# VectorE's order behind the next unit's maxima, and half of a layer's maxima moved into its attention

## The chip, the cores and the metric

The kernel runs on one core of a Trainium2 chip. A core has five engines with a queue each: TensorE (PE for its matmuls, PEld for the loads of their stationary operand), VectorE (DVE), ScalarE (ACT), GpSimd (POOL) and SyncE (SP). SP and POOL also issue the DMAs here. The metric is the device time in microseconds; the kernel before takes 2418.72 us, the median of three runs (2417.28 to 2425.54).

## The reference

Four blocks of attention, one after the other, work on x, 4 sequences of 1024 tokens with 256 channels, and on a context of 4 times 77 tokens. All is float32.

- L0 (16 heads of 16 channels): layer norm, self attention under a mask, residual; layer norm, attention to the context, residual; layer norm, a feed-forward of 1024 channels with relu, residual. Under the mask only a few keys at the end of a sequence take part.
- L1 (4 heads of 64 channels), three layers: the first attends to the context, the second and third to x itself, 1024 queries by 1024 keys. Each is

```
Q, K, V = relu(q @ Wq + bq), relu(k @ Wk + bk), relu(v @ Wv + bv)
attn    = softmax(Q K^T / 8) * query_mask
out     = layer_norm(attn V + q)
x       = leaky_relu(out @ Wff + bff, 0.2) + out
```

- L2 and L3 (16 heads of 16 channels): attention to the context, residual and layer norm; L2 has an output projection, L3 has none.

A softmax needs the maximum of each row of scores before the exponentials.

## The kernel before

**Items and units.** Each layer is run for one sequence after the other; a layer and a sequence is an item. Seven layers make 28 items: `SelfFew` (self attention of L0, when at most 32 keys count), `Cross16` (attention to the context with 16 heads: "ca" of L0, "l2", "l3"), `Cross4` (first layer of L1), `Self4` (second and third layer of L1). An item's attention is a row of units: 4 in SelfFew, 8 in Cross16 and Cross4, 16 in Self4.

**The order of PE.** PE runs in the order in which the program is written. That order is made by `Pipe` and `Pump`. In each unit `Pipe.unit` calls what is due as "full", then the unit's scores, then what is due as "next", then the pump, then what is due as "turn", "late" and "col". The pump fills a unit with steps from two lists: the first holds the start of the next item (norms, transposes to channels, queries, maxima), the second the end of the item before (projection, residual, norm, feed-forward). Each step has a cost of about its PE time, a lag (so much other cost shall pass before the list's next step) and at times a test. `Pump.__call__` takes the list that is further behind, and stops when the unit has its share or when neither list is ready. In an item's last unit it takes all that is left, lags or not. `Pump.until` takes steps of the first list, without regard to lags, until a test holds: an item's attention calls it before the units of each half of the tokens, so that the half's start is there. The other engines have no written order: a planner puts each of their instructions in a queue's order, by when it finds them ready and by the order of the program.

**Self4, the stage from 930 to 1884 us.** A unit is 128 queries and a pair of heads against 1024 keys. `Self4.scores`: PE writes two score tiles `ss` (two PSUM banks each; there are two such buffers, so the next unit's scores wait until this unit's are read), DVE takes the negative maximum of each (line 1241), ACT the exponentials with it into PR (line 1247). PR has two buffers, and each holds a pair of units. `turned_by_blocks` is called as "next", one unit later: DVE transposes the unit's part of PR in blocks of 32 by 32 (line 1259), and after the second unit of a pair 16 DMAs, 8 on SP's queue and 8 on POOL's, move the blocks into PT (line 1266). Two and three units after that `weighted` multiplies with V (line 1302) from PT.

**Cross16.** An item's `start` makes a list: for each half c of the tokens a norm where the layer has one, two transposes (`turn`), two queries, eight `maxima` (line 270 on PE into two PSUM tiles, line 275 on DVE), then `shift`. A maximum is needed per head and query so that the exponentials cannot overflow; `shift` splits it into three bf16 parts with four DVE instructions (lines 304 to 307) and lets PE transpose these (line 310), whose copy SH is added into the scores by a small matmul (line 352). `have_half` then counts the half. The scores of a unit are lines 346 and 352, the exponentials 356, the weighting 365, the transposes back 377. The PSUM pool "p1" for all these small tiles has four buffers. `SelfFew` inherits `shift` and has its own maxima (lines 917 and 921). The normalized x lies in a tile of tag "F", of which there is one; norms of both lists use it.

Of the kernel before, what the change touches and what calls it, by code (L numbers as in the profile page):

```python
# [13 lines left out]
ALU = mybir.AluOpType  # L14
# [69 lines left out]
class Pump:  # L84
# [31 lines left out]

    def until(self, test):
        while not test():
            self.take(0)


class Pipe:
# [26 lines left out]
    def run(self, items):  # L149
        pump = Pump(self, 1, items[0].start(), [])  # L150
        pump.until(lambda: items[0].halves >= 1)
        left = pump.lists[0]
        before = None
        for a, b in zip(items, items[1:]):
            b.prev = a
        for i, item in enumerate(items):
            last = i + 1 == len(items)
            first = left + ([] if last else items[i + 1].start())
            second = (before.end() if before else []) + (item.end() if last else [])
            left = []  # L160
            idle = item.idle()
            self.pump = pump = Pump(self, item.units + idle, item.more() + first, second)
            for _ in range(idle):
                self.unit()
            for scores in item.attend():
                self.unit(scores, item.cost)
            before = item
        while self.due:
            pump.n = 0
            self.unit()  # L170
        pump.n = pump.units - 1
        pump()


class Item:
# [4 lines left out]

    def more(self):

        return []

    def idle(self):

# [2 lines left out]
    def __init__(self, net, layer, b):  # L189
        self.net, self.l, self.b = net, layer, b  # L190
        self.halves, self.ended = 0, 0
        self.prev, self.later_half = None, True

    def room(self):

# [9 lines left out]
class Cross16(Item):  # L205
# [7 lines left out]
    def start(self):  # L213
# [23 lines left out]
        def norm(c):  # L237
            if l.norm is None:
                self.xn = x[:, 4 * c : 4 * c + 4, :]
                return  # L240
            mv, rstd = self.mv, self.rstd
            self.xn = net.tile("F", [P, 4, C], name="xn")
            for i in range(4):
                t = 4 * c + i
                nc.vector.tensor_scalar(
                    self.xn[:, i, :], x[:, t, :], mv[:, t, 0:1], rstd[:, t : t + 1], ALU.subtract, ALU.mult
                )

        def turn(c, cc):
            pt = net.p1.tile([P, 512], F32, tag="p1", name="pt")  # L250
            for i in range(4):
                nc.tensor.transpose(pt[:, ts(i, P)], self.xn[:, i, ts(cc, P)], net.ident)
            at = None if l.norm is None else COL_LN + 4 * (l.norm - 1) + cc
            g, be = (None, None) if at is None else (net.cols[:, at : at + 1], net.cols[:, at + 2 : at + 3])
            net.evac(self.hT[:, cc, ts(c, 512)], pt, g, be)

        def query(e, c):
            pp = net.p1.tile([P, 512], F32, tag="p1", name="pp")
# [19 lines left out]

        ln = l.norm is not None
        step(0, new, lag=8 * ln)  # L280
        for c in range(2):
            step(0, norm, c, lag=3 * ln)
            step(0.5, turn, c, 0)
            step(0.5, turn, c, 1, lag=2)
            if c == 0:
                step(0, new_q, test=self.room)
            for e in range(2):
                step(1.8, query, e, c)
            for e in range(2):
                for i in range(4):  # L290
                    step(0.55, maxima, e, 4 * c + i, lag=3 if (e, i) == (1, 3) else 0)
            step(0.3, self.shift, c)
            step(0, self.have_half)
        return steps

    def shift(self, c):

        net, h = self.net, H16
        nc = net.nc
        m = self.mx[:, 4 * c : 4 * c + 4, :].rearrange("p t (j g) -> p t j g", j=4)  # L300
        m3, rest = net.m3[c], net.rest16[c]
        parts = [m3.rearrange("p t (j r) -> p t j r", j=4)[:, :, :, i : 3 * G : 3] for i in range(3)]
        left = rest.rearrange("p t (j g) -> p t j g", j=4)
        nc.vector.tensor_copy(parts[0], m)
        nc.vector.tensor_tensor(left, m, parts[0], ALU.subtract)
        nc.vector.tensor_copy(parts[1], left)
        nc.vector.tensor_tensor(parts[2], left, parts[1], ALU.subtract)
        pm = net.p1.tile([P, 512], BF16, tag="p1", name="pm")
        for i in range(4):
            nc.tensor.transpose(pm[:, ts(i, P)], m3[:, i, :], net.identb)  # L310
        net.evac(self.sh[:, c, :], pm)

    def shift_by_row(self, c):
# [217 lines left out]
class Feed:  # L531
# [15 lines left out]
    def steps(self, b):  # L547
# [9 lines left out]

        def norm(c):
            s["xn"] = net.tile("F", [P, 4, C], name="xn")
            for i in range(4):  # L560
                t = 4 * c + i
                nc.vector.tensor_scalar(
                    s["xn"][:, i, :], x[:, t, :], s["mv"][:, t, 0:1], s["rstd"][:, t : t + 1], ALU.subtract, ALU.mult
                )

        def turn(c, cc):
# [2 lines left out]
                nc.tensor.transpose(pt[:, ts(i, P)], s["xn"][:, i, ts(cc, P)], net.ident)  # L569
            at = COL_LN + 8 + cc  # L570
            net.evac(s["hT"][:, cc, ts(c, 512)], pt, net.cols[:, at : at + 1], net.cols[:, at + 2 : at + 3])

        def hidden(q, f):

# [28 lines left out]
            step(0, self.load)  # L603
        step(0, new, lag=8)
        for c in range(2):
            step(0, norm, c, lag=3)
            step(0.5, turn, c, 0)
            step(0.5, turn, c, 1, lag=2 * c)
        for q in range(4):
# [24 lines left out]
class Self16(Cross16):  # L634
# [8 lines left out]
    def start(self):  # L643
# [18 lines left out]

        def norm(c):
            self.xn = net.tile("F", [P, 4, C], name="xn")
            net.normal(self.xn, x, self.mv, self.rstd, c)

        def turn(c, cc):
            net.turn_normal(self.hT, self.xn, 1, c, cc)

        def query(g, c):  # L670
            pp = net.p1.tile([P, 512], F32, tag="p1", name="pp")
# [49 lines left out]
        step(0, new, lag=8 if b else 0)  # L721
        for c in self.cs:
            if b:
                step(0, norm, c, lag=3)
                step(0.5, turn, c, 0)
                step(0.5, turn, c, 1, lag=2)
            step(1.8, query, 0, c)
# [100 lines left out]
class SelfFew(Cross16):  # L828
# [5 lines left out]
    def start(self):  # L834
# [21 lines left out]

        def norm(c):
            self.xn = net.tile("F", [P, 4, C], name="xn")
            net.normal(self.xn, x, self.mv, self.rstd, c)

        def turn(c, cc):
            net.turn_normal(self.hT, self.xn, 1, c, cc)

        def query(e, c):
            pp = net.p1.tile([P, 512], F32, tag="p1", name="pp")
# [57 lines left out]
        step(0, new, lag=8 if b else 0)  # L923
        for c in self.cs:
            if b:
                step(0, norm, c, lag=3)
                step(0.5, turn, c, 0)
                step(0.5, turn, c, 1, lag=2)
            if c == 1:
# [3 lines left out]
            if c == 1:  # L933
                step(0.9, values)
            for t in range(4 * c, 4 * c + 4):
                step(0.9, maxima, t, lag=3 if t % 4 == 3 else 0)
            step(0.3, self.shift, c)
            step(0, self.have_half)
        return steps
# [149 lines left out]
class Self4(Item):  # L1089
# [133 lines left out]
    def scores(self, p, t):  # L1223
# [14 lines left out]
        for h in range(2):  # L1238
            at = slice(2 * p + h, 2 * p + h + 1)
            s2 = ss[h].rearrange("p k n -> p (k n)")  # L1240
            nc.vector.tensor_reduce(self.nm[:, t, at], s2, AX.X, ALU.max, negate=True)  # L1241
            if net.blocks:
                out = self.pr[:, t % 2, h, :].rearrange("p (c k i) -> p k c i", c=4, i=32)
                s2 = s2.rearrange("p (k c i) -> p k c i", c=4, i=32)
# [8 lines left out]
    def turned_by_blocks(self, p, t, pr):  # L1253
# [2 lines left out]
        net = self.net  # L1256
        nc = net.nc
        part = pr[:, t % 2].rearrange("p h s -> p (h s)")
        nc.vector.transpose(part, part)  # L1259
        if t % 2 == 0:  # L1260
            return

# [189 lines left out]
class Net:  # L1452
    def __init__(self, ctx, tc, t):
        self.ctx, self.tc, self.nc, self.t = ctx, tc, tc.nc, t
        self.flip = 0

    def evac(self, out, src, scale=None, bias=None):

# [694 lines left out]
```

## Time and profile before

The profiled execution took 2419.14 us, with a span of 2417.3 us from its first to its last instruction, and a mean granted clock of PE of 0.951.

| stage, us from the start | length | PE busy | DVE busy | ACT busy | PE clock | DMA share |
|---|---|---|---|---|---|---|
| 0 to 40: load, first norm | 40 | 13.10 | 19.85 | 8.33 | 0.81 | 0.47 |
| 40 to 244: SelfFew | 204 | 182.59 | 127.31 | 42.52 | 0.97 | 0.09 |
| 244 to 686: Cross16 "ca" and feed-forward | 442 | 423.00 | 202.73 | 134.05 | 0.99 | 0.03 |
| 686 to 930: Cross4, with the last feed-forward | 244 | 216.96 | 135.78 | 108.14 | 0.91 | 0.02 |
| 930 to 1884: Self4, two layers | 954 | 902.51 | 782.49 | 445.23 | 0.97, 0.98 | 0.65, 0.69 |
| 1884 to 2417: Cross16 "l2" and "l3" | 533 | 458.28 | 313.93 | 190.62 | 0.89 | 0.05 |

Busy time is the union of an engine's instructions in microseconds. PE's is not work at full pace: the end of a matmul is modelled, so one that waits inside counts as busy. A line of the profile names the source line, the engine and the operation, the tiles as out<-in, the number of instructions, then their busy time, the mean of one in ns, and the idle time of the engine before them with what ended it. A line of the waits names who waited, for whom, how long in all, how often and the longest. The clock is the share of full speed that PE was granted.

### The profile page before, as it was taken

How to read it: one execution, taken by the hardware profiler on the slowest of the kernel's cores; microseconds unless marked ns; L12 is line 12 of the kernel's file. 1: busy time of each engine (PE TensorE's matmuls, PEld its weight loads, DVE VectorE, ACT ScalarE, POOL GpSimd, SP SyncE). 2: the span in 40 equal slices, each digit the busy share in tenths (PEclk: the TensorE clock that was granted, in tenths of full speed). 3: DMA queues.
4: the chain of work that ended last, by engine and by line, in shares of the span. 5: the costliest groups of instructions: out<-in, count | busy, mean ns of one | idle time of the engine just before them, and what ended most of it. 6: DMA issues, size and time to landing. Idle time of an engine off the chain costs nothing. (4 is left out here: it accounts for less than half of the span.)

```text
span 2417.3 us, 31250 instructions
## 1 busy us (share of the span) xinstructions
PE 2196.4 (91%) x11035; PEld 1226.0 (51%) x11035; DVE 1582.1 (65%) x3170; ACT 928.9 (38%) x1828; POOL 382.3 (16%) x652
## 2 busy tenths in 40 slices
PE   4899999999999979999998999999999899898886
PEld 2556546666768645545443545444444444444331
DVE  5566655444233666888889688878887655655665
ACT  1222342222332545544444445444443343333333
POOL 2000000000000000333333233333232100000000
PEclk8999999999989989999999999999999898998888
DMA  4000010000000001677667576666785300000000
GB/s 128 18 1 16 5 35 1 1 7 5 7 5 3 1 5 34 149 160 151 144 144 159 120 149 146 148 148 146 154 156 111 70 5 1 5 1 1 27 18 28
DMA packets 148550, 158.01 MB, mean 65 GB/s; under 512 B 51489, under 2 KB 130658, under 8 KB 148386
## 3 DMA queue, kind: packets, MB, share of 16 engines
q1 hardware_dynamic: 121842, 85.31, 16.6%
q0 software_dynamic: 25488, 69.56, 12.8%
q8 instruction: 91, 1.49, 0.3%
q10 hardware_dynamic: 1056, 1.05, 0.1%
q14 instruction: 73, 0.60, 0.1%
HBM read 17.41 MB, written 4.19 MB: 9 GB/s over the span
## 5 line engine op out<-in xcount | busy, mean ns | idle before, releaser
L1247 ACT ACTIVATE PR<-ss,nm 128x1024 f32<-128x1024 f32 x256 | 284.8, 1114 | 381.1 <-DVE nm L1241 294.4
L1259 DVE STREAM_TRANSPOSE PR<-PR 128x2048 f32<-128x2048 f32 x128 | 295.8, 2311 | 130.4 <-ACT PR L1247 115.5
L1266 POOL DMA_DIRECT2D PT<-PR x512 | 279.8, 554 | 591.9 <-PE ss L1230 227.9
L1230 PE MATMUL ss<-QK 64*128 64x512 f32 x1024 | 322.9, 630 | 26.3 <-ACT PR L1247 26.1
L1241 DVE TENSOR_REDUCE nm<-ss 128x1 f32<-128x1024 f32 x256 | 299.7, 1210 | 20.0 <-PE ss L1230 19.9
L1302 PE MATMUL po<-PT,V 128*64 128x256 f32 x2048 | 252.4, 389 | 2.3 <-DVE mx L275 2.2
L356 ACT ACTIVATE PT<-pb 77x1024 f32<-77x1024 f32 x192 | 185.4, 1016 | 178.4 <-PE pb L352 178.4
L275 DVE TENSOR_REDUCE mx<-pa 128x4 f32<-128x308 f32 x384 | 156.0, 469 | 71.2 <-PE pa L270 70.6
L1230 PEld LDWEIGHTS ss<-QK 64*128 64x128 f32 x1024 | 112.7, 188 | 172.0 <-ACT PR L1247 94.5
L270 PE MATMUL pa<-KA,QT 64*128 64x308 f32 x768 | 167.2, 490 | 30.2 <-DVE mx L275 29.8
L1302 PEld LDWEIGHTS po<-PT,V 128*64 128x64 f32 x2048 | 137.1, 138 | 106.1 <-issue 46.3
L365 PE MATMUL po<-PT,Vc 77*32 77x512 f32 x768 | 136.8, 652 | 18.5 <-ACT PT L356 9.6
L270 PEld LDWEIGHTS pa<-KA,QT 64*128 64x128 f32 x768 | 101.5, 197 | 97.3 <-DVE mx L275 45.4
L1509 POOL TENSOR_TENSOR pw<-va,minus_half 128x4 f32<-128x4 f32 (+1 forms) x28 | 38.0, 1358 | 619.7 <-DVE va L1507 542.0
L1469 ACT COPY OT<-po 128x512 f32<-128x512 f32 x57 | 33.4, 587 | 231.2 <-PE po L365 217.5
L346 PE MATMUL pb<-QT,KA 32*77 32x512 f32 x768 | 114.5, 668 | 0.0
L595 PE MATMUL pp<-w,hid 128*128 128x256 f32 x512 | 114.0, 381 | 0.0
L580 PE MATMUL pp<-hF,w 128*128 128x256 f32 x512 | 113.2, 379 | 0.0
L595 PEld LDWEIGHTS pp<-w,hid 128*128 128x128 f32 x512 | 96.5, 190 | 15.9 <-DVE mx L275 2.5
L580 PEld LDWEIGHTS pp<-hF,w 128*128 128x128 f32 x512 | 97.1, 190 | 14.6 <-issue 1.3
L1500 DVE BATCH_NORM_STATS2 st<-x 128x6 f32<-128x256 f32 x256 | 97.7, 405 | 5.6 <-DMA x<-in_x 4.4
L1373 PE MATMUL pp<-wo,hE 128*128 128x256 f32 x384 | 96.4, 393 | 1.6 <-ACT hE L1476 1.5
(257 smaller groups left out, 3147.3 us busy)
## 6 DMA issues: line engine op xcount, KB each, us to landing
PT<-PR SPq DMA_DIRECT2D x512, 128.0 KB, 5.5
PT<-PR POOLq DMA_DIRECT2D x512, 128.0 KB, 4.6
x<-in_x SPq DMA_DIRECT2D x4, 1024.0 KB
out<-x SPq DMA_DIRECT2D x8, 512.0 KB, 2.9
w<-in_ff_w SPq DMA_DIRECT2D x2, 1024.0 KB
gb<-in_norms POOLq DMA_DIRECT2D x5, 256.0 KB, 7.2
wk<-in_l_wk SPq DMA_DIRECT2D x10, 128.0 KB
wv<-in_l_wv SPq DMA_DIRECT2D x5, 256.0 KB, 3.5
```

The source lines that it names most:

```text
L270: nc.tensor.matmul(pas[i], self.qt[rows, e, ts(t, P)], self.ka[rows, e, :, :], start=True, stop=True)
L275: nc.vector.tensor_reduce(out, pas[i].rearrange("p (j s) k -> p j s k", s=2), AX.X, ALU.max, negate=True)
L356: nc.scalar.activation(pt[:, 2 * i : 2 * i + 2, :], pbs[i][:SC], AF.Exp, scale=self.l.scale)
L365: nc.tensor.matmul(po[ts(j, h.slot), :], l.v[:, self.b, col : col + h.vw], pt[:, j, :], start=True, stop=True)
L580: nc.tensor.matmul(pp[:, i, :], self.w1[:, cc, ts(f + i, P)], s["hT"][:, cc, ts(q, 2 * P)], start=cc == 0, stop=cc == NC - 1)
L595: nc.tensor.matmul(pp[:, u, :], s["a"][:, f, ts(u, P)], self.w2[:, f, :], start=f == 0, stop=f == NF - 1)
L1230: nc.tensor.matmul(ss[h][:, k, :], self.qk[p][rows, 0, ts(t, P)], self.qk[p][rows, 1, ts(k, 512)], start=True, stop=True,)
L1241: nc.vector.tensor_reduce(self.nm[:, t, at], s2, AX.X, ALU.max, negate=True)
L1247: nc.scalar.activation(out, s2, AF.Exp, bias=self.nm[:, t, at], accum_out=self.sums[:, t, at])
L1259: nc.vector.transpose(part, part)
L1266: (nc.sync, nc.gpsimd)[a % 2].dma_start(out=pt[ts(c, 32), :, :, a].rearrange("p t h k j -> p (t h) (k j)"), in_=pr[ts(a, 32), :, :, ts(c, ...
L1302: nc.tensor.matmul(po[64 * h : 64 * h + 64], self.v[:, k, 64 * (2 * p + h) : 64 * (2 * p + h) + 64], pts[:, :, h, :, k, :] if net.blocks e ...
```

## The change

1. **The tie.** The second of a unit's two maxima is kept as `net.reduced`, and the block transposes are issued under an order that puts them behind it in DVE's queue. When they are called, it is the maxima of the unit after.
2. **Context layers of 16 heads.** The list of `start` now has the transposes and queries of both halves first, the queries of the second half set between the maxima of the first; the second half's maxima and shift go into a list `rest`, which `more` hands to the pump at the head of the first list in the item's own attention. Each maximum has a lag of 0.5.
3. **The split of the shift.** The four DVE instructions become a step `thirds` of their own ahead of `shift`, with the lag between them; in SelfFew too (there with a lag of 3, which before stood between the last maximum and the shift).
4. **The flag.** `held` is set with each norm into tag "F" and cleared with its second transpose; a norm waits by its test until it is clear, and `until` may take the second list's step when the first list's is not allowed.

```diff
     def until(self, test):
         while not test():
-            self.take(0)
+            first = self.lists[0][0]
+            self.take(0 if first.test is None or first.test() or not self.lists[1] else 1)
...
     def more(self):
-        return []
+        return self.rest
...
         ln = l.norm is not None
         step(0, new, lag=8 * ln)
-        for c in range(2):
-            step(0, norm, c, lag=3 * ln)
+        def turns(c):
+            step(0, norm, c, lag=3 * ln, test=net.not_held if ln else None)
             step(0.5, turn, c, 0)
             step(0.5, turn, c, 1, lag=2)
-            if c == 0:
-                step(0, new_q, test=self.room)
-            for e in range(2):
-                step(1.8, query, e, c)
+
+        turns(0)
+        step(0, new_q, test=self.room)
+        for e in range(2):
+            step(1.8, query, e, 0)
+        turns(1)
+        self.rest = Steps()
+        for c in range(2):
+            step = (steps, self.rest)[c].add
             for e in range(2):
                 for i in range(4):
-                    step(0.55, maxima, e, 4 * c + i, lag=3 if (e, i) == (1, 3) else 0)
+                    step(0.55, maxima, e, 4 * c + i, lag=0.5)
+                if c == 0 and e == 0:
+                    step(1.8, query, 0, 1)
+            step(0, self.thirds, c, lag=2)
+            if c == 0:
+                step(1.8, query, 1, 1)
             step(0.3, self.shift, c)
             step(0, self.have_half)
         return steps
 
-    def shift(self, c):
-
-        net, h = self.net, H16
+    def thirds(self, c):
+
+        net = self.net
         nc = net.nc
         m = self.mx[:, 4 * c : 4 * c + 4, :].rearrange("p t (j g) -> p t j g", j=4)
...
         nc.vector.tensor_copy(parts[1], left)
         nc.vector.tensor_tensor(parts[2], left, parts[1], ALU.subtract)
+
+    def shift(self, c):
+
+        net = self.net
+        nc = net.nc
         pm = net.p1.tile([P, 512], BF16, tag="p1", name="pm")
         for i in range(4):
-            nc.tensor.transpose(pm[:, ts(i, P)], m3[:, i, :], net.identb)
+            nc.tensor.transpose(pm[:, ts(i, P)], net.m3[c][:, i, :], net.identb)
         net.evac(self.sh[:, c, :], pm)
...
             self.xn = net.tile("F", [P, 4, C], name="xn")
+            net.held = True
...
             for t in range(4 * c, 4 * c + 4):
-                step(0.9, maxima, t, lag=3 if t % 4 == 3 else 0)
+                step(0.9, maxima, t)
+            step(0, self.thirds, c, lag=3)
             step(0.3, self.shift, c)
             step(0, self.have_half)
...
-            nc.vector.tensor_reduce(self.nm[:, t, at], s2, AX.X, ALU.max, negate=True)
+            net.reduced = nc.vector.tensor_reduce(self.nm[:, t, at], s2, AX.X, ALU.max, negate=True)
...
         part = pr[:, t % 2].rearrange("p h s -> p (h s)")
-        nc.vector.transpose(part, part)
+        with net.tc.issue_after(net.reduced.ins):
+            nc.vector.transpose(part, part)
         if t % 2 == 0:
             return
```

More of the change, by code (lines that the diff above doesn't have):

```diff
@@ L166, in run @@
                 self.unit(scores, item.cost)
+            assert last or not any(pump.lists)
             before = item
@@ L192, in __init__ @@
         self.prev, self.later_half = None, True
+        self.rest = []
     def room(self):
@@ L255, in turn @@
             net.evac(self.hT[:, cc, ts(c, 512)], pt, g, be)
+            if cc and at is not None:
+                net.held = False
         def query(e, c):
@@ L559, in norm @@
             s["xn"] = net.tile("F", [P, 4, C], name="xn")
+            net.held = True
             for i in range(4):
@@ L571, in turn @@
             net.evac(s["hT"][:, cc, ts(c, 512)], pt, net.cols[:, at : at + 1], net.cols[:, at + 2 : at + 3])
+            if cc:
+                net.held = False
         def hidden(q, f):
@@ L605, in steps @@
         for c in range(2):
-            step(0, norm, c, lag=3)
+            step(0, norm, c, lag=3, test=net.not_held)
             step(0.5, turn, c, 0)
@@ L664, in norm @@
             self.xn = net.tile("F", [P, 4, C], name="xn")
+            net.held = True
             net.normal(self.xn, x, self.mv, self.rstd, c)
@@ L668, in turn @@
             net.turn_normal(self.hT, self.xn, 1, c, cc)
+            if cc:
+                net.held = False
         def query(g, c):
@@ L723, in start @@
             if b:
-                step(0, norm, c, lag=3)
+                step(0, norm, c, lag=3, test=net.not_held)
                 step(0.5, turn, c, 0)
@@ L858, in norm @@
             self.xn = net.tile("F", [P, 4, C], name="xn")
+            net.held = True
             net.normal(self.xn, x, self.mv, self.rstd, c)
@@ L862, in turn @@
             net.turn_normal(self.hT, self.xn, 1, c, cc)
+            if cc:
+                net.held = False
         def query(e, c):
@@ L925, in start @@
             if b:
-                step(0, norm, c, lag=3)
+                step(0, norm, c, lag=3, test=net.not_held)
                 step(0.5, turn, c, 0)
@@ L1455, in __init__, with not_held @@
         self.flip = 0
+        self.held = False
+    def not_held(self):
+        return not self.held
     def evac(self, out, src, scale=None, bias=None):
```

## The prediction

> **What bounds the kernel now.** I read the table of engines first, then the windows by stage, then the waits, then the order of time on VectorE in the stage that has the block transposes.
>
> ```profile
> PE 2196.4 (91%) x11035; PEld 1226.0 (51%) x11035; DVE 1582.1 (65%) x3170; ACT 928.9 (38%) x1828; POOL 382.3 (16%) x652
> ```
> ```profile
> 244.00:686.00 442.00, 423.00 (x2272) 281.29 (x2270) 202.73 (x517) 134.05 (x192) 16.76 (x19) 0.99 0.03 9
> ...
> 930.00:1400.00 470.00, 444.27 (x2111) 219.54 (x2111) 379.09 (x480) 228.77 (x484) 141.27 (x254) 0.97 0.65 138
> 1400.00:1884.00 484.00, 458.24 (x2232) 226.58 (x2230) 403.40 (x523) 216.46 (x428) 153.82 (x274) 0.98 0.69 147
> 1884.00:2417.00 533.00, 458.28 (x2642) 217.62 (x2638) 313.93 (x842) 190.62 (x244) 33.63 (x39) 0.89 0.05 14
> ```
> The columns are the length, then busy time of PE, PEld, DVE, ACT, POOL, the granted clock, DMA share, GB/s. PE looks full everywhere, but in the two L1 self layers (930 to 1884 us) DVE is busy 782 of 954 us, and in the last stage PE is idle 75 us at a clock of 0.89. The waits tell who holds whom:
>
> ```profile
> ACT PR L1247 <- DVE nm L1241: 294.4, 94, 7.9
> ...
> DVE PR L1259 <- ACT PR L1247: 115.5, 87, 2.1
> ...
> PEld ss L1230 <- ACT PR L1247: 94.5, 123, 2.4
> ...
> PEld L310 <- DVE m L307: 46.1, 17, 4.6
> PEld pa L270 <- DVE mx L275: 45.4, 36, 5.5
> ...
> PE pm L310 <- DVE m L307: 37.2, 17, 3.9
> ```
> ACT waits for maxima, DVE for ACT's exponentials, PE for the PSUM that they free: a ring. VectorE in order of time, over one unit:
>
> ```profile
> 1117.84 2.35 DVE L1241 TENSOR_REDUCE nm<-ss 128x1 f32<-128x1024 f32 x2
> 1121.45 2.31 DVE L1259 STREAM_TRANSPOSE PR<-PR 128x2048 f32<-128x2048 f32 x1 [1.27 <-ACT PR L1247]
> 1123.69 0.65 DVE L1379 TENSOR_TENSOR low<-pp,low 128x512 f32<-128x512 f32 x1
> 1124.38 0.69 DVE L1380 TENSOR_TENSOR x<-low,x 128x512 f32<-128x512 f32 x1
> ```
> Maxima 2.35, idle 1.27 for the exponentials of the same unit, their transpose 2.31, other work 1.3, and the next maxima at 1124.99: 7.15 us. All 128 transposes stand so, directly behind their own unit's maxima. The sum 2.35 + 1.27 + 2.31 + other work is the unit's time, which is 113.04/16 = 7.07 and 117.06/16 = 7.32 in two whole items (windows of 1407.02 to 1520.06 and 1162.55 to 1279.61): I use 7.2. PE's stall hides in its matmuls:
>
> ```profile
> L1230 PE MATMUL ss<-QK 64*128 64x512 f32 x1024 | 322.9, 630 | 26.3 <-ACT PR L1247 26.1
> ```
> A unit's eight records take 1.99 us where nothing holds them (1107.03), and 3.04 where they wait for the second bank (1099.94). 322.9 - 128 x 1.99 = 68 us are waits inside the matmuls, with 26 idle before them: 94 us that PE loses to this ring.
>
> **Part 1, the tie.** No instruction is added or removed; each transpose goes behind the next unit's two maxima. What falls out of the ring is the 1.27 idle and the 2.31 transpose between maxima. Four things can then be last:
> - DVE without idle: 2.35 + 2.31 + 1.4 = 6.1 a unit.
> - The chain maxima, exponentials, scores: exponentials end 3.5 after the maxima start (1117.84 to 1121.33), the next scores and their maxima 2.36 later (1136.10 to 1138.46): 5.9.
> - PE: 1.99 + 4.05 = 6.04 in plain units (1122.21 to 1128.25), some 6.3 on average.
> - The buffers PR. There are two, each for a pair of units; the exponentials of the pair after next wait until the 16 DMAs (8 of SP's queue, 8 of POOL's) have read one. These DMAs are moved too: they follow the pair's second transpose.
>
> ```profile
> 1123.80:1136.30 12.50, 10.46 (x59) 5.46 (x57) 9.42 (x10) 7.50 (x19) 4.38 (x8) 1.00 0.83 169
> 1136.30:1138.50 2.20, 2.20 (x9) 0.96 (x10) 2.20 (x2) 0.26 (x2) 0.00 (x0) 1.00 0.00 0
> ```
> The transpose ends at 1123.76; the DMAs run until 1136.3, and then there is none. Over the steady pairs their last packet ends 11.1 to 13.0 us after the transpose, about 11.7. Now the exponentials that need the buffer come 14 to 18 us after it, so nobody waits. Tied, the transpose ends 2.35 + 2.31 = 4.7 us after the maxima of the following unit start instead of before them. From there: 4.7 + 11.7 + 0.1 = 16.5 until the exponential of the unit two later may start; 4.65 from its start to the next unit's maxima (2.24 for both exponentials, 0.05, 2.36); 6.3 of PE's pace to the maxima after those: 27.4 us for four units, 6.9 each, against 4 x 7.2 = 28.8. So the buffer's loop is the new bound, above PE's 6.3. It gives 1.4 x 32 = 45 us. I take 35: two of 16 units carry 6 us of other PE work (8.06 from 1114.15 to 1122.21) and shrink little, and other DVE work of 0.6 to 0.7 a piece will at times stand ahead of a maximum. Bounds: 94 gained if the buffers do not bind; 47 lost if the loop is longer (rival 2).
>
> Behind the maxima that now wait for PE stand the transpose, then the DMAs on SP and POOL; behind these on POOL the 1.0 us powers (L1353), whose readers have a lag of 5. The weighting matmuls start 15 to 18 us after the transpose today, 3 to 6 after the last packet; the shift eats that, but they wait for the same DMAs as the exponentials and stand 2 to 4 us later in PE's order, so they are covered; if not, 1 us for each of 64 pairs. At a layer's end the last maxima are the unit's own and the tie asks nothing.
>
> The Trainium skill's page "Perfetto Trace Analysis", section "Optimization Strategy", speaks against a reordering: the same bubble repeating on the engine that should be full can mean too few buffers for the next tile, which no order of VectorE mends. By it this part is worth little; the rows above put that buffer loop at 27.4 of 28.8. The page "DMA: Bandwidth & Descriptors", section "Where 436 GB/s comes from", lets SBUF-to-SBUF moves run near 435 GB/s, an estimate of 4.8 us for the 2.1 MB; the loop would then be 20.5 and PE alone the bound. The row has 169 GB/s.
>
> **Part 2, the context layers.** Per item nothing is added but one ordering: four casts and subtractions ("thirds", 1.0 us of DVE: 0.24, 0.23, 0.24, 0.29) leave the step of their transposes, and eight of 16 maxima with the second shift move into the item's own attention. PE idles today before L310 and L270. In the last stage these two are 41 us (16.1 and 24.7), in 244 to 686 another 9; half-clock matmuls after such idles (L365 1.93 at 2168.49 against 1.07) add perhaps 10. A stall before L310 is 1.9 us: last maximum, thirds, transposes back to back.
>
> After: the first half's thirds have a query (1.8 us of PE) before the shift, which hides 1.0 us. The second half must be done at unit 4 of 8. A maximum has a lag of 0.5, so where the other list has no costed step (l3) a unit takes one maximum: four of eight are left at unit 4 and taken at once, 4 x 0.94 of DVE + 1.0 + 0.4 against 4 x 0.8 + 0.4 of PE, some 2 us idle. In l2 and ca the other list fills the lag; at most one maximum and a shift are left, again 1.9. So of two stalls an item one goes, and L270's waits, which come from eight maxima in a row behind the last layer's norms, shrink by half at best: 8 items of l2 and l3 at 2 us, ca 4 in all: -20. Bounds: -60 (all of 50 and the clock's 10), +16 if each of the 8 items only gains the stall at unit 4.
>
> At the border, l2's first item also leaves eight maxima (7.5 us of DVE) out of the last self item, whose ring is DVE's: 0 to -7, taken as 0, since its first list still drains there.
>
> SelfFew gets the same split: nothing. Its stalls (PE idle 1.91 at 92.53, 103.93, 144.11, 157.21) lie where the last unit drains its list without lags, so thirds and shift stay adjacent; bounds 0 to -15 (the eight stalls). The flag "held" and the change in "until" issue nothing; a normalization held back lets the other list go, and without such a list would cost its 4 x 0.36.
>
> **Sum.** The profiled execution took 2419.1 (span 2417.3), the median of three is 2418.7, the same within noise. -35 - 20 = -55: 2364.
>
> **Rivals.**
> 1. The buffers do not bind (DMAs under 10 us when they start elsewhere, or exponentials late enough): -94 - 20, 2305. For it: DMA share only 0.69 over an item. Against: 11 us or more in every steady pair.
> 2. Slower: VectorE is FIFO, and the other work of a unit (1.4) slips between maxima and transpose, or ahead of the maxima. The loop meets that queue three times in four units; twice is 2.8, 27.4 + 2.8 = 30.2, +1.4 x 32 = +45, less 20: 2444. It decides from 1.4 us on (2.0 with part 2's gain). For it: rows of 2.4 to 2.9 us of such work in single units; against: the transpose's data is long ready when the maxima end.
> 3. The loop gives back just what the tie gains, and the context layers move their stalls (L310's 1.9 from the end of an item to unit 4): 2399 to 2422. For it: 1.4 of 28.8 is thin.
> 4. The tie does nothing because the order is such already: excluded, all 128 transposes precede the next maxima.
>
> **How the numbers follow.** Forecast 0.42; rival 1 0.16; rival 2 0.24; rival 3 0.18, of which 0.08 lie within 0.3% (7 us, what a measurement of this kernel can tell), 0.07 below and 0.03 above. Faster 0.65, same 0.08, slower 0.27. The likeliest one's own range is 2330 to 2395. The range reaches to 2296 (rival 1 with 9 us more of part 2) and to 2444, leaving half of rival 2 and a little of rival 1 outside.
>
> **What would show it.** Right: on VectorE maxima, maxima, transpose of the unit before; L1259's idle for ACT (115.5) gone; L1230 nearer 255 than 322.9; ACT's L1247 or PE's L1302 waiting for the DMAs of PR, tens of us, where now it is 29.2. Rival 1: no such wait, and units of 6.3. Rival 2: units over 7.2 with other work between L1241 and L1259. Part 2: L310's 37.2 halved, idle at 1.9 before unit 4 of each l3 item, clock over 0.89 at the end. Wrong would be a DMA wait that also holds ACT's evacuations and empties PE's PSUM.

## The result and the profile after

The changed kernel takes 2443.15 us, the median of six runs (2433.97 to 2456.53); the kernel before took 2419.16 us in the runs beside it (2416.13 to 2425.54). The ratio is 1.0098, with a 95% interval of 1.0076 to 1.0119: slower by one per cent, where 2364 was forecast. The profiled execution took 2443.2 us, with a span of 2441.3.

Where it went is read stage by stage. The stages in the next tables are cut at the first scores of each kind of layer (Self4 ends at its last scores), so that they hold the same units in every kernel; PE idle is the length less PE's busy time, and "half clock" is the time for which the clock record of the trace shows 0.50.

| stage, us | before: length, PE idle, half clock | after |
|---|---|---|
| SelfFew | 218.9, 20.8, 6.8 | 206.9, 16.5, 3.4 |
| ca | 411.9, 14.2, 6.8 | 448.3, 24.1, 47.8 |
| Cross4 | 252.6, 27.0, 44.4 | 249.6, 26.4, 41.0 |
| Self4 | 944.6, 51.5, 44.4 | 954.6, 89.9, 78.5 |
| l2 | 267.0, 24.5, 32.6 | 268.0, 20.3, 30.7 |
| l3 | 247.0, 45.6, 72.9 | 235.9, 33.6, 44.0 |

The other 75 us, ahead of SelfFew and between Self4 and l2, grew by 2.4. Two stages lose much, ca (36.4) and Self4 (10.0); SelfFew (12.0), l3 (11.1) and Cross4 (3.0) gain. The windows of the kernel after, cut as in the prediction (length, then PE, PEld, DVE, ACT, POOL busy, clock, DMA share, GB/s), show the first of these as a lower clock, and Self4 as a PE less busy in a longer stage:

```profile
244.00:712.00 468.00, 443.37 (x2265) 274.65 (x2264) 204.40 (x522) 134.75 (x192) 15.49 (x19) 0.95 0.03 8
...
955.00:1917.00 962.00, 872.12 (x4287) 448.55 (x4287) 775.66 (x981) 448.01 (x908) 296.21 (x527) 0.96 0.66 140
1917.00:2441.00 524.00, 468.71 (x2690) 213.95 (x2686) 325.05 (x864) 192.13 (x246) 33.55 (x39) 0.92 0.07 16
```

The costliest groups of the kernel after (busy time, mean ns of one, idle before and what ended it):

```profile
L1334 PE MATMUL po<-PT,V 128*64 128x256 f32 x2048 | 271.0, 410 | 68.4 <-DMA PT<-PR 48.3
L1261 PE MATMUL ss<-QK 64*128 64x512 f32 x1024 | 291.1, 632 | 10.8 <-ACT PR L1278 10.3
L1291 DVE STREAM_TRANSPOSE PR<-PR 128x2048 f32<-128x2048 f32 x128 | 294.4, 2300 | 0.0
```

VectorE does what was asked: 127 of the 128 transposes now stand behind the next unit's two maxima, and the 115.5 us for which they waited for ACT are gone. The scores fell from 322.9 to 291.1, so the old ring is open. In its place stands a wait that was not in the list of before: the weighting matmuls wait for the DMAs from PR to PT. Their line in the kernel before had almost no idle time:

```profile
L1302 PE MATMUL po<-PT,V 128*64 128x256 f32 x2048 | 252.4, 389 | 2.3 <-DVE mx L275 2.2
```

One turn of the new ring, in order of time (VectorE, PE and ACT of the kernel after):

```profile
1477.26 2.35 DVE L1272 TENSOR_REDUCE nm<-ss 128x1 f32<-128x1024 f32 x2 [0.84 <-PE ss L1261]
...
1479.53 2.30 DVE L1291 STREAM_TRANSPOSE PR<-PR 128x2048 f32<-128x2048 f32 x1
...
1494.82 1.11 ACT L1278 ACTIVATE PR<-ss,nm 128x1024 f32<-128x1024 f32 x1 [1.14 <-DMA PT<-PR]
1495.15 2.79 PE L1334 MATMUL po<-PT,V 128*64 128x256 f32 x16 [1.98 <-DMA PT<-PR]
...
1497.87 2.35 PE L1261 MATMUL ss<-QK 64*128 64x512 f32 x6
```

and the DMAs between, as two windows of the same kernel:

```profile
1481.83:1493.74 11.91, 11.34 (x54) 6.08 (x52) 11.77 (x25) 4.83 (x10) 5.47 (x9) 1.00 0.83 178
1493.74:1494.82 1.08, 0.00 (x0) 0.00 (x0) 1.08 (x2) 0.00 (x1) 0.00 (x0) 1.00 0.00 0
```

The transpose ends at 1481.83, the last packet at 1493.74; then nothing is on the DMAs for 1.08 us, and only then the exponential starts and, at 1495.15, the weighting. PE has no work at all in that last window. The next scores stand behind the weighting and start at 1497.87. The sixteen weighting matmuls take 2.79 us here, and 1.95 in most units: the clock record shows 0.50 from 1496.1 to 1499.5. Of the 78.5 us at half clock in Self4 most are such single stretches of 3.4 us.

### The profile page after: what moved, and what is told of

Its sections match the earlier page's. It is cut to its first block, busy times and chain, and to the rows that moved or that the text cites. A ratio compares the mean times of both kernels' runs of the same rounds, so it can differ in the third digit from the quotient of the medians.

```text
span 2441.3 us, 31308 instructions
## 1 busy us (share of the span) xinstructions
PE 2195.3 (90%) x11035; PEld 1217.0 (50%) x11035; DVE 1586.7 (65%) x3170; ACT 934.3 (38%) x1828; POOL 382.0 (16%) x652
## 3 DMA queue, kind: packets, MB, share of 16 engines
q1 hardware_dynamic: 121842, 85.31, 16.4%
## 5 line engine op out<-in xcount | busy, mean ns | idle before, releaser
L1298 POOL DMA_DIRECT2D PT<-PR x512 | 278.9, 552 | 586.7 <-issue 127.9
L1272 DVE TENSOR_REDUCE nm<-ss 128x1 f32<-128x1024 f32 x256 | 300.8, 1215 | 73.0 <-PE ss L1261 72.9
L1334 PE MATMUL po<-PT,V 128*64 128x256 f32 x2048 | 271.0, 410 | 68.4 <-DMA PT<-PR 48.3
L1261 PE MATMUL ss<-QK 64*128 64x512 f32 x1024 | 291.1, 632 | 10.8 <-ACT PR L1278 10.3
L1334 PEld LDWEIGHTS po<-PT,V 128*64 128x64 f32 x2048 | 151.4, 144 | 174.1 <-issue 113.2
L281 DVE TENSOR_REDUCE mx<-pa 128x4 f32<-128x308 f32 x384 | 161.1, 469 | 80.1 <-PE pa L276 79.4
L276 PE MATMUL pa<-KA,QT 64*128 64x308 f32 x768 | 167.5, 483 | 13.1 <-DVE mx L281 10.4
L386 PE MATMUL po<-PT,Vc 77*32 77x512 f32 x768 | 143.5, 653 | 5.1 <-ACT PT L377 3.9
L276 PEld LDWEIGHTS pa<-KA,QT 64*128 64x128 f32 x768 | 84.0, 191 | 96.4 <-issue 33.3
L604 PE MATMUL pp<-hF,w 128*128 128x256 f32 x512 | 118.6, 386 | 0.0
L619 PEld LDWEIGHTS pp<-w,hid 128*128 128x128 f32 x512 | 97.0, 190 | 16.5 <-issue 2.2
L1405 PE MATMUL pp<-wo,hE 128*128 128x256 f32 x384 | 96.5, 393 | 1.6 <-ACT hE L1512 1.5
L266 PE MATMUL pp<-hT,wq 128*128 128x512 f32 x192 | 93.1, 618 | 5.1 <-ACT hT L1507 4.5
```

The lines of the kernel that those rows point to most:

```text
L276: nc.tensor.matmul(pas[i], self.qt[rows, e, ts(t, P)], self.ka[rows, e, :, :], start=True, stop=True)
L281: nc.vector.tensor_reduce(out, pas[i].rearrange("p (j s) k -> p j s k", s=2), AX.X, ALU.max, negate=True)
L386: nc.tensor.matmul(po[ts(j, h.slot), :], l.v[:, self.b, col : col + h.vw], pt[:, j, :], start=True, stop=True)
L604: nc.tensor.matmul(pp[:, i, :], self.w1[:, cc, ts(f + i, P)], s["hT"][:, cc, ts(q, 2 * P)], start=cc == 0, stop=cc == NC - 1)
L619: nc.tensor.matmul(pp[:, u, :], s["a"][:, f, ts(u, P)], self.w2[:, f, :], start=f == 0, stop=f == NF - 1)
L1261: nc.tensor.matmul(ss[h][:, k, :], self.qk[p][rows, 0, ts(t, P)], self.qk[p][rows, 1, ts(k, 512)], start=True, stop=True,)
```

## The experiments

Ten kernels were run. The two parts of the change were first taken apart, each with one run that takes away the suspected cause; then came the controls and the combinations. Unless a row says otherwise, stage times and waits are those of each kernel's profiled execution, and ratios are to the kernel before on the same chip. A stage of the same code differs between these executions: ca takes 411.6 to 411.9 us in the five kernels that have the code of before there, but l3 243.0 to 252.3 in them, and 231.3 to 242.9 in the six that have the change's l3.

| kernel | median us | ratio, 95% interval | ca: length, half clock | Self4: length, PE idle |
|---|---|---|---|---|
| before | 2421 to 2422 | 1 | 411.9, 6.8 | 944.6, 51.5 |
| tie alone | 2438.52 | 1.0066 (1.0045 to 1.0088) | 411.6, 10.2 | 958.4, 87.2 |
| context layers alone | 2413.49 | 0.9970 (0.9950 to 0.9990) | 445.3, 37.5 | 927.3, 48.2 |
| context layers, lag 0 | 2390.29 | 0.9861 (0.9844 to 0.9877) | 411.4, 0.0 | 938.9, 51.1 |
| tie, DMAs by unit | 2370.62 | 0.9774 (0.9755 to 0.9793) | 411.6, 10.2 | 890.2, 35.6 |
| DMAs by unit, no tie | 2423.02 | 1.0000 (0.9985 to 1.0015) | 411.7, 10.2 | 942.0, 52.7 |
| tie, weighting later | 2461.43 | 1.0176 (1.0154 to 1.0199) | 411.8, 6.8 | 979.1, 67.9 |
| context, filler in ca | 2414.87 | 0.9973 (0.9957 to 0.9988) | 444.8, 20.5 | 930.3, 47.4 |
| change, DMAs by unit | 2362.12 | 0.9772 (0.9750 to 0.9795) | 438.2, 17.1 | 874.7, 30.0 |
| the same, lag 0 in ca and l2 | 2337.72 | 0.9660 (0.9637 to 0.9683) | 413.1, 3.4 | 893.4, 40.7 |
| the same, lag 0 in ca alone | 2326.63 | 0.9618 (0.9602 to 0.9634) | 411.4, 0.0 | 875.1, 30.6 |

### The tie alone

```diff
-            nc.vector.tensor_reduce(self.nm[:, t, at], s2, AX.X, ALU.max, negate=True)
+            net.reduced = nc.vector.tensor_reduce(self.nm[:, t, at], s2, AX.X, ALU.max, negate=True)
...
-        nc.vector.transpose(part, part)
+        with net.tc.issue_after(net.reduced.ins):
+            nc.vector.transpose(part, part)
```

> The tie alone, with the context layers as before. If the tie costs by the loop through the two PR buffers (in the profile after, maxima to maxima over four units 29.0 us where 28.4 stood before), this run is 5 to 14 us slower than before, all of it between the first and the last scores of the self layers, and PE waits for the DMAs ahead of the weighting matmuls by some 50 us. If the loss in that stage came from the context layers (other steps on VectorE at its borders), the run is as fast as before or faster, 2390 to 2420.

It lost 16.5 us, a little more than expected, and 13.8 of them in Self4. The tie by itself is a loss: PE's idle in Self4 rose from 51.5 to 87.2 us, and the half clock there from 44.4 to 68.3. SelfFew, whose code is the same, took 3.1 us more in this execution, with 13.0 us at half clock instead of 6.8.

### The context layers alone

The change without its tie:

```diff
-        with net.tc.issue_after(net.reduced.ins):
-            nc.vector.transpose(part, part)
+        nc.vector.transpose(part, part)
```

> All of the change but the tie. If the loss before the self layers is the context layers' own, ca takes 20 to 26 us more, l2 and l3 8 to 12 less, the self layers nothing: 2428 to 2438. If the two parts only lose together, 2400 to 2415.

It gained 8.5 us, so the parts have opposite signs. The time lies in the second of the expected ranges, but the loss of ca, which the first one assumed, is there and larger. The sum hides larger terms: SelfFew 218.9 to 208.6, ca 411.9 to 445.3, Self4 944.6 to 927.3, l3 247.0 to 237.4. Of the 17 us of Self4, 15 come from its last item (129.2 to 114.2), in whose time the start of l2 is made.

### The context layers, with no lag between the maxima

On top of the kernel of the section before:

```diff
-                    step(0.55, maxima, e, 4 * c + i, lag=0.5)
+                    step(0.55, maxima, e, 4 * c + i)
```

> As the run without the tie, and the maxima have no lag of 0.5. In the profile after, three maxima and the shift are forced at unit 4 of each ca item, PE idles 2.2 to 2.9 us there and then runs 7 to 20 us at half clock. If that stall is the cause, maxima without a lag are done before unit 4, the half clock between 244 and 712 us falls from 48 us to under 15, and the run takes 2400 to 2415. If the loss lies in the order of the lists (units 4 to 6 without steps to fill them), ca stays 20 us longer and the run at 2428 to 2440.

ca falls back to 411.4 us, and the whole to 2390.29, below the expected range: l2 is 10.6 us shorter than with the lag too, while Self4 (11.6) and l3 (12.1) are longer. With a lag of 0.5 three maxima, the thirds and the second shift are left when the fourth unit has passed, and `until` takes them at once. In the order of time of the kernel after, at the first such place:

```profile
355.04 0.22 DVE L320 CAST m<-mx 128x64 bf16<-128x64 f32 x1
...
355.44 0.42 DVE L1536 BATCH_NORM_STATS2 st<-x 128x6 f32<-128x256 f32 x1
...
356.20 0.27 DVE L323 TENSOR_TENSOR m<-rest,m 128x64 bf16<-128x64 f32 x1
...
356.54 0.61 PE L331 MATMUL pm<-identb,m 128*128 128x128 bf16 x4 [2.91 <-DVE mv L1537]
...
357.07 2.01 PE L367 MATMUL pb<-QT,KA 32*77 32x512 f32 x8
```

The thirds stand between the statistics of the item before on VectorE, PE idles 2.91 us, and the scores after it take 2.01 us instead of the 1.10 they take at full clock (375.23). The window of the same kernel behind that idle:

```profile
356.53:373.20 16.67, 16.50 (x68) 4.90 (x68) 6.70 (x23) 5.97 (x8) 2.13 (x2) 0.50 0.13 45
```

Three units run there bare, with nothing from the pump, at half clock. The loss of ca closes as a sum. Between the runs with lag 0.5 and with lag 0 it is 33.9 us; PE's idle differs by 25.0 - 9.9 = 15.1, and 37.5 us at half clock cost half of that, 18.8: together 33.9.

### ca with more work for PE

Also made to the change without its tie; the added transposes compute nothing that is used:

```diff
+        if c == 1 and self.l.ff is not None:
+            idle = net.p1.tile([P, 512], F32, tag="p1", name="idle")
+            for i in range(20):
+                nc.tensor.transpose(idle[:, ts(i % 4, P)], net.ident, net.ident)
         for i in range(4):
             nc.tensor.transpose(pm[:, ts(i, P)], net.m3[c][:, i, :], net.identb)
```

> The change without the tie (2413.49 us) with 20 further transposes of the identity into a tile that nobody reads, put on PE ahead of the second shift of each ca item, where PE stands idle 2.2 to 2.9 us before three unfilled units; they compute nothing. Theory 'the clock is halved by the idle and the bare units behind it': the half-clock time in ca falls from 37.5 us to under 20, and ca from 445 us to 425 to 440, though work was added. Rival 'the stall is only an idle, and the half clock comes from the bare units alone': the half-clock time stays between 30 and 50 us and ca within 3 us of 445.

The half clock fell from 37.5 to 20.5 us, as the clock theory has it, while ca's length stayed (445.3, 444.8), as the rival has it. At the second item the filler now stands where PE was idle (order of time of this kernel):

```profile
484.05 2.40 PE L332 MATMUL idle<-ident 128*128 128x128 f32 x20
...
487.03 0.40 PE L335 MATMUL pm<-identb,m 128*128 128x128 bf16 x4 [0.58 <-DVE mv L1540]
487.36 1.10 PE L371 MATMUL pb<-QT,KA 32*77 32x512 f32 x8
```

and the scores behind it run at full pace. My expectation had not put the filler's own work on the bill: 4 x 2.40 = 9.6 us, against 17/2 = 8.5 of clock and 2.2 of idle won. That sums to -1.1 for a measured -0.5. Paying the idle with dummy work gains nothing. The fall of the total does not show that the idle brings the half clock, since the same code without the filler has 47.8 us (the change), 37.5 (without its tie) and 17.1 (the change with each unit's own DMAs, below). The places say more. These three kernels have nine such idles of 2.2 to 2.9 us in ca, and a stretch of half clock, 3.4 to 20.5 us long, begins at eight of them, at most 1.7 us after the idle's end; with the filler none begins within 7 us of these places. So the idle ahead of the bare units takes part in the half clock. What sets the length of a stretch, and what the bare units add, is open.

### The tie, with each unit's own DMAs

```diff
         if t % 2 == 0:
-            return
-
-        pt = net.tile("B", [P, 2, 2, 4, NT, 32], name="PT")
+            self.pt = net.tile("B", [P, 2, 2, 4, NT, 32], name="PT")
+        pt = self.pt
...
-                    out=pt[ts(c, 32), :, :, a].rearrange("p t h k j -> p (t h) (k j)"),
-                    in_=pr[ts(a, 32), :, :, ts(c, 256)].rearrange("p t h n -> p (t h) n"),
+                    out=pt[ts(c, 32), t % 2, :, a].rearrange("p h k j -> p h (k j)"),
+                    in_=pr[ts(a, 32), t % 2, :, ts(c, 256)],
...
+        if t % 2 == 0:
+            return
+
```

> The tie alone, and each unit's half of PR is moved by DMAs of its own right after its own transpose (32 of 64 KB for a pair instead of 16 of 128 KB). If the buffer loop is what takes the tie's gain, the last packet lands 6 to 8 us after the pair's second transpose instead of 11.7, the loop falls to 24 or 25 us for four units, PE no longer waits for these DMAs, and the run takes 2350 to 2395. If VectorE's order itself costs (other work queued behind the waiting maxima), it stays at 2422 to 2435. If the 32 issues choke SP's queue (0.8 us each), it is over 2440.

The lines of the tie, as above, come with it. Half of PR leaves one unit earlier. The groups of this kernel and its Self4 as one window, beneath each other:

```profile
L1230 PE MATMUL ss<-QK 64*128 64x512 f32 x1024 | 286.2, 619 | 10.3 <-ACT PR L1247 9.7
L1305 PE MATMUL po<-PT,V 128*64 128x256 f32 x2048 | 255.8, 393 | 1.8 <-ACT hE L1479 1.3
```

```profile
944.30:1834.50 890.20, 854.62 (x4307) 435.24 (x4307) 779.16 (x998) 441.44 (x903) 553.00 (x1031) 0.98 0.59 153
```

The idle before the weighting, 68.4 us in the kernel after and 56.4 with the tie alone, is 1.8. Four units take 26.8 us (24 or 25 were expected), and Self4 is 54 us shorter than before and 68 shorter than with the tie alone. POOL is busy for nearly twice the time in Self4 (295.1 to 553.0), off the path here.

### Each unit's own DMAs, without the tie

The edit of the section before without the lines of the tie, made to the kernel before.

> The kernel before, with each unit's half of PR moved by 16 DMAs of its own, without the tie. A control for the run of 2370.62 us that had both. Theory 'the buffer's loop binds only where the tie stands': before the tie the exponentials that need a buffer come 14 to 18 us after the transpose, later than the DMAs of a pair end (11.7), so earlier DMAs free nothing that anybody waits for: 2410 to 2430, and the idle of L1259 for ACT stays at some 115 us. Rival 'the smaller DMAs are the gain and the tie is worth nothing': near 2370.

Nothing changes, 1.0000, and VectorE's wait for the exponentials of its own unit stays (104.9 us, 115.5 before). The smaller DMAs alone are worth nothing, the tie alone costs 16.5 us, and the two together gain 51. Without the tie VectorE's ring binds, with it the buffers' loop does; one edit alone opens one of the two.

### The tie, with the weighting a unit later

```diff
-            net.pipe.later("turn", 2 + half, lambda half=half: self.weighted(p, t, pt, half, state))
+            net.pipe.later("turn", 3 + half, lambda half=half: self.weighted(p, t, pt, half, state))
```

> The tie alone, with the weighting one unit later (three and four units after the pair's DMAs instead of two and three). It tells which of the two waits on the DMAs' last packet holds the tied loop. Theory 'the weighting's wait': PE stops at the first weighting matmul and the next scores stand behind it, so taking it out of the way lets the next scores start 1.2 us earlier in four units at most: 0.6 to 1.2 us x 29 less than the tie's 2438.5, 2404 to 2421, and PE's idle before the weighting (54.6 us by 'issue') all but gone. Rival 'the exponentials' wait for PR': the scores wait for the PSUM that these free, the stall only moves from the weighting's line to the scores': 2430 to 2442.

Neither held: 2461, slower than both ranges. In the steady pairs the rival's mechanism is seen. The waits of PE in the run with the tie alone:

```profile
PE po L1303 <- DMA PT<-PR: 39.7, 20, 3.1
...
PE ss L1230 <- ACT PR L1247: 8.7, 12, 1.5
```

and in this one:

```profile
PE ss L1230 <- ACT PR L1247: 44.5, 32, 3.6
```

The first line is gone and the second has grown by nearly as much; the scores' busy time, which holds waits inside the matmuls, grew from 287.0 to 329.7 as well. The next scores start 1.1 us earlier (19.1 after the maxima instead of 20.2), and four units still take 29.25 us (29.35 with the tie alone). The rest of the loss is elsewhere: the item at the end of each layer takes 135.4 and 134.4 us instead of 127.9 and 126.2, and the first one 117.2 instead of 112.3. A pair's PT is held one unit longer, which would explain a stop where a layer begins, but this was not tried by itself. Self4 also ran 102.4 us at half clock, 68.3 with the tie alone; what came first there is open.

### The change, with each unit's own DMAs

The same edit, made to the kernel after.

> The change as it was made (lag 0.5 everywhere), with each unit's half of PR moved by its own DMAs and nothing else. The buffer's loop and the context layers' lags were undone in one run together; this one undoes the loop alone. If the terms are separate: Self4 falls from 954.6 to about 890, the time from 2443 to 2370 to 2383, with ca at 448 and its half clock near 48 us as before. If the last self item also gains what it gained without the tie: 2362 to 2372.

Self4 takes 874.7 us and the whole 2362, the second of the two cases. ca still loses (438.2), so the two causes are separate. The half clock in ca was 17.1 us here and 47.8 in the kernel after, though the code of that stage is the same. The last self item takes 108.4 us, against 124.0 with the tie and these DMAs alone.

### The change, with each unit's own DMAs and other lags

Lag 0 in ca and l2 and 0.5 in l3, and each unit's own DMAs as above:

```diff
-                    step(0.55, maxima, e, 4 * c + i, lag=0.5)
+                    step(0.55, maxima, e, 4 * c + i, lag=0.5 if l.name == "l3" else 0)
```

> The whole change, with each unit's half of PR moved by its own DMAs and with the maxima's lag at 0 in ca and l2 and at 0.5 in l3. If the terms add up: Self4 as in the run with the tie and the unit's DMAs (890 us, 54 less than before), SelfFew 207 with ca 411 (12 less together), l2 256 (11 less), l3 237 (10 less): 2422 - 87 = 2335, range 2322 to 2350. If the shorter self units leave the last layers' lists less room, or clock lost in one stage comes back in the next, 2350 to 2370.

The terms add up: 2337.72. But the last self item took 127.4 us here, where the seven before it take 103 to 117. In the next run the lag is 0 in ca alone:

```diff
-                    step(0.55, maxima, e, 4 * c + i, lag=0.5 if l.name == "l3" else 0)
+                    step(0.55, maxima, e, 4 * c + i, lag=0 if l.name == "ca" else 0.5)
```

> The whole change with each unit's own DMAs and the maxima's lag at 0 in ca alone, at 0.5 in l2 and l3 (the run of 2337.72 us had 0 in l2 too). Asked: whether l2's first item, which now leaves eight maxima out of the last self item also in lag, shortens that item (127.4 us there; the seven before it take 103 to 117). Theory 'the last self item is VectorE's again once the buffers don't bind, so the maxima taken out of it count': it falls by 10 to 15 us as in the run without the tie (129.2 to 114.2), l2 is 10 to 12 us longer, the sum within 6 us of 2337. Rival 'under the tie VectorE's work in that item is hidden': the item stays at 124 to 128, l2 is 10 to 12 longer, 2345 to 2352.

That item fell to 109.0 and l2 grew by 10.5 us. The total, 2326.63, is lower than expected: l3 was 3 us shorter too, which is within the spread of that stage. Both kernels leave the second half's eight maxima out of that item, which ends at its last scores. With lag 0 the other eight come in lumps, two in each of units 11 and 12 and four in unit 14 (counted from 0), and these units take 11.9, 13.3 and 12.4 us; with lag 0.5 each of the units 11 to 14 gets one and takes 5.2 to 6.6, and the other four come behind the last scores. So the lag that costs 34 us in ca earns 18 at the border of Self4. This version beats both kernels, 3.8% below the one before. Its ca and its Self4 as windows:

```profile
266.30:677.70 411.40, 401.50 (x2190) 263.18 (x2189) 183.75 (x467) 128.69 (x185) 13.42 (x16) 1.00 0.03 9
```

```profile
928.00:1803.20 875.20, 844.63 (x4265) 429.00 (x4263) 770.93 (x977) 439.95 (x901) 547.55 (x1024) 0.98 0.60 154
```

ca runs at full clock, and PE is busy 96.5% of Self4 (94.5% before, 90.6% with the change).

## Why the prediction was wrong

**The tie: the mechanism was right, the sum 1.7 us short.** The forecast was that the buffers PR become the bound. They did. The step that failed is "27.4 us for four units, 6.9 each, against 4 x 7.2 = 28.8". The chain, counted from the start of the maxima that now stand ahead of the transpose; the right column holds medians over the 42 steady pairs of the kernel after:

| step | predicted | measured |
|---|---|---|
| transpose ends | 4.7 | 4.57 |
| last DMA packet ends | 16.4 | 16.0 |
| exponential starts | 16.5 | 17.3 |
| scores of the next unit start | 18.8 | 20.1 |
| their maxima start | 21.2 | 22.4 |
| maxima after those start | 27.4 | 29.1 |

The DMAs' 11.7 us was well measured. Three terms were not: of the 1.7 us 0.8 stand at the exponential, 0.5 at the scores, and the last step, for which I took PE's pace of 6.3, takes 6.7. From the last packet to the exponential I took 0.1 us; it is 1.1 (median of the 35 pairs of the kernel after in which ACT had nothing else before it; 0.66 to 1.37 in the middle eight tenths). The trace of before does not show this hand-over plainly: exponentials wait for these DMAs in nine places there (29.2 us in all), and in each of them other packets run until 0.04 us or less before the exponential starts. The Trainium skill's "DMA: Bandwidth & Descriptors", section "Anatomy of one DMA — SWDGE (gpsimd) path", gives a DMA some 2 us of fixed cost and puts most of it behind the last byte, on the receipt ahead of the semaphore; the 1.1 us here, on DMAs of which half are GpSimd's and half SP's, agree in kind. The prediction named the page for its bandwidth of near 435 GB/s, where the rows have 169 and 178, and not for its latency.

The second term is the weighting. "They wait for the same DMAs as the exponentials and stand 2 to 4 us later in PE's order, so they are covered" was wrong: PE reaches them before the data is there, in the turn shown 1.98 us early, and the scores of the next unit stand behind their 1.95 us (2.79 in that turn). The fallback of 1 us for each of 64 pairs had the right size, and I did not carry it into the sum. Moving the weighting showed that this is no loss on top: without it the scores wait as long for the exponentials.

So four units take 29.1, where the kernel before takes 28.4 in the same measure (not 28.8): 0.7 x 32 = 23 us lost by the medians of the steady pairs, 13.8 measured with the tie alone. Over all stretches of four units the mean goes from 29.66 to 30.06 there, which is 0.40 x 31 = 12. Part of the loss can be the clock, which the sum did not have: 24 us more at half clock in Self4 are at most 12 us at half the pace, and no run separates them from the waits. Rival 3, "the loop gives back just what the tie gains", comes nearest, on the wrong side of zero. Rival 2's sign and size came out (2444 against 2443.15) for a reason that was not its own: the transpose ends 4.57 us after the maxima start and the next maxima follow the start of their scores by 2.3 us, as without a queue, so no other work slips in at either place. That it came out was luck. Rival 1 fell. One reading behind these sums was too strong: all 128 transposes of the kernel before stand ahead of the next unit's maxima, but only 71 stand "directly behind their own unit's maxima"; between the others stands other work of VectorE.

The page cited against the reordering, "Perfetto Trace Analysis", section "Optimization Strategy", reads a repeated bubble as a possible lack of buffers for the next tile. The runs agree with half of it: freeing PR earlier without the reordering gave 1.0000, the reordering without it 1.0066, both 0.9774.

**Part 2: -20 forecast, -8.5 alone.** Four terms were wrong, and they cancel in part.

- "ca 4 in all" is the large one: ca lost 33.4. The step that failed is "In l2 and ca the other list fills the lag; at most one maximum and a shift are left": in ca three maxima were left, with the thirds and the shift, and in l2's first item four. I priced the stall at unit 4 at 1.9 us; it was up to 2.9 in ca, since VectorE has the norm statistics of the item before in its queue just there. I gave the clock a value only as a gain in the last stage, and did not ask what a new idle does to it where the units behind are bare.
- "So of two stalls an item one goes, and L270's waits ... shrink by half at best": PE's own waits for L270's maxima fell from 29.8 to 10.4 us, more than half, and those before the shift did not halve: 37.2 before, 32.8 and 5.8 after (behind the thirds and behind the statistics). In l3 the result is -11.1, in l2 +1.0.
- "SelfFew gets the same split: nothing." Its six stalls are unchanged, but its last unit, which drains ca's first list, now has eight maxima where it had sixteen (32 and 64 matmuls before ca's first scores); that unit takes 21.8 us instead of 32.2 up to these scores, and the stage is 12 us shorter.
- "0 to -7, taken as 0" for the last self item: -15.0 without the tie, -3.1 with it (126.2 to 123.1). VectorE's work counts there only while VectorE binds; under the tie the DMAs do, and once these are taken out of the way by each unit's own DMAs, the same work counts again (124.0 to 108.4). This is most of why the parts do not add: the spans of the profiled executions change by +20.0 and -6.3 alone and by +24.0 together, 10.3 more than the sum (16 by the medians of the runs). In this item alone the difference is 11.9 (-3.0 and -15.0 alone, -6.1 together).

**The rest.** The range, 2296 to 2444, held the time at its very end. Of the signs named to be looked for, these came out: maxima, maxima, transpose on VectorE; L1259's idle gone; the DMA wait in tens of us; a clock over 0.89 at the end (0.92). Two did not: L1230's line, at 291.1, lies nearer to 322.9 than to 255 (287.0 with the tie alone, barely the other way), and L310's 37.2 was not halved. The first three show a loop that binds and cannot tell 27.4 from 29.1, which was the whole question.

## What to carry to other kernels

When an order is changed so that one ring opens, write down the next ring with every hand-over in it, the time from a DMA's last packet to its reader included, and compare it with the old one measured in the same way; a margin of 1.4 us in 28.8 says nothing before that. If the next ring is a buffer, free it in smaller pieces in the same edit: here each half was worth nothing or less alone, and the two together 2.3%. Deferred work needs slack where it lands: eight maxima moved into an item gained 12 us where they came from and cost 34 with a lag of 0.5, where a deadline met a busy VectorE and units without filling.

## What was not expected of the hardware

- An idle of PE of 2.91 us was followed by 17 us at a clock of 0.50, in which the records show PE busy for 16.50 of 16.67 us; waits inside matmuls count as busy there, and the records do not tell how much they are. The Trainium skill's "TensorE: Matmul & The Clock Gate", section "What's actually happening", lowers the clock after an idle window of about 3.4 us and restores it after a busy one of that length. The idle ahead of this stretch was shorter than that, and the busy time did not restore it for five such lengths. The half clock comes in steps of 3.4 us in this record, which agrees with the page's window.
- The same code in ca spent 47.8, 37.5 and 17.1 us at half clock in three kernels that differ only outside that stage; at half the pace that is a spread of 15 us. The idle of 2.91 us in the first item is the same in all three, and 17.1, 3.4 and 10.2 us at half clock follow it.
- Between the last DMA packet and the instruction that waits for it lie 1.1 us in which neither the DMAs nor, in the turn shown, PE have any work.
